# Interleaving the down products of two token tiles, and moving one subtraction from GpSimd to VectorE

## The chip, the core and the metric

The kernel runs on one core of a Trainium2 chip. A core has five engines with instruction queues of their own: TensorE (PE; its weight loads are listed apart as PEld), VectorE (DVE), ScalarE (ACT), GpSimd (POOL) and SyncE (SP), which here issues DMA transfers. Each engine takes its instructions in the order in which the program emits them and waits on semaphores for the others. The metric is the device time of one execution in microseconds (us), the median over the runs.

## What is computed

Four sequences of 512 tokens with 512 features; all in float32. For each sequence the features are normalised, and two branches read the result: attention with 16 heads of 32 (with RMS norm and rotation of queries and keys), and a gated feed-forward layer with 1408 hidden units. They are multiplied at the end:

```python
xn = _layernorm(x, axis=-1)
s = _L0_attn_ref(xn, L0_attn_w_qkv, L0_attn_w_out, L0_attn_q_gamma, L0_attn_k_gamma)
g = _silu(_L0_ffn_ref(xn, L0_ffn_wq_gate, L0_ffn_s_gate, L0_ffn_wq_up, L0_ffn_s_up, L0_ffn_wq_down, L0_ffn_s_down))
x = x + s * g
...
def _L0_ffn_ref(x, wq_gate, s_gate, wq_up, s_up, wq_down, s_down):
    gate = _qlinear(x, wq_gate, s_gate)
    gate = jax.nn.silu(gate)
    up = _qlinear(x, wq_up, s_up)
    return _qlinear(gate * up, wq_down, s_down)
```

The mask of the attention is causal. The feed-forward weights are integers, less a zero point and times a scale per row (`_qlinear`).

## The kernel before

The work is cut into 16 units (b, g): sequence b of 4 and head group g of 4 heads. The 11 hidden blocks of 128 are shared out over the four groups of a sequence: two to group 0, three to each of the others (`chunks`). A unit has two stages. The first, `hidden_window`, makes the unit's hidden blocks: for every block the gate product and the up product (`hidden`, L583, eight matmuls each), then `gate` and `gated`. Between them it does what is left of the last unit's attention, and in group 3 it turns the next sequence's normalised x. The second stage is the attention of the unit, and with it the down products of the blocks just made, one for each of the four token tiles of 128. The attention stage comes in three versions: `attention_window` for the first three units, `placed_window` for the next twelve, `last_window` for the last.

The order of the work is written out by hand: every engine's queue is the order of the calls, and nothing is moved afterwards. In the attention stage `s[t]` is the attention of token tile t. `scores` (L450) fills four PSUM banks; `probabilities` takes on VectorE the minimum of a row (L471) and on ScalarE the exponential (L481). `turn` transposes the probabilities on TensorE (L497) with a copy behind it (L125 on ScalarE, L127 on VectorE), `blocks` and `spread` do it with VectorE (L514) and DMA (L528). `values` (L537) multiplies by v. `fresh` is the projection of the next unit: `product` (L368), then `rotate`, which starts with two operations on ScalarE (L379, L380), goes on with four on VectorE (L400 to L407) and ends on GpSimd (L408, L314, L315, L410).

A float32 operand that is multiplied at the faster format is kept as two parts, a high half (rounded) and a low half (the rest). The hidden value has them in `h[:, i, 0]` and `h[:, i, 1]`. For one block, `gated` multiplies on VectorE (L600), makes the high half on ScalarE (L601) and the low half on GpSimd (L602). A down product of one token tile (`contract`, L612) is two matmuls per block, high then low, summed in one PSUM bank of 512 columns; `add` on VectorE (L623 for group 0, L625 for the others) adds the bank to `acc`. The first token tile uses the pool `ps_d`, of one bank, and so do the third and fourth; the second uses a bank of the pool of transposes (`bank_t`, two banks in turn). `contract` and the `add` that it returns are called separately, so that other work can stand between them.

The next sequence's x is cut in the same way into `xh` and `xl` by `Norm.cut`: ScalarE makes the high half (L350), another engine the low half (L351). It is called tile by tile through `halves`, in the attention stage of group 3 of sequences 0, 1 and 2. In `placed_window` GpSimd makes the low halves of tiles 0 and 1, VectorE those of 2 and 3.

Of the kernel before, what the change touches and what calls it, by code (L numbers as in the profile page):

```python
# [11 lines left out]
F32 = mybir.dt.float32  # L12
# [9 lines left out]
P = 128  # L22
B, N, D = 4, 512, 512
# [3 lines left out]
NC = D // P  # L27
# [24 lines left out]
def interleaved(  # L52
# [27 lines left out]
    nc = tc.nc  # L80
# [14 lines left out]
    ps_d = ctx.enter_context(tc.tile_pool(name="ps_d", bufs=1, space=PSUM))  # L95
# [8 lines left out]
    def bank_t(name):  # L104
        return ps_t.tile([P, 512], F32, tag="t", name=name)
# [33 lines left out]
    chunks = [list(range(first))] + [list(range(first + 3 * g, first + 3 * g + 3)) for g in range(NC - 1)]  # L139
# [42 lines left out]
    wdT = const.tile([P, NF, D], F32R, name="wdT")  # L182
# [50 lines left out]
    loaded, turning, finished = [], [], set()  # L233
# [74 lines left out]
    h = seq.tile([P, FC, 2, N], F32R, name="h")  # L308
# [288 lines left out]
    def gated(sil, f, bank, to):  # L597
# [3 lines left out]
        nc.scalar.copy(to[:, 0, :], sil)  # L601
        nc.gpsimd.tensor_tensor(to[:, 1, :], sil, to[:, 0, :].bitcast(F32), ALU.subtract)  # L602

    def contract(b, g, t, other=False):

        name = f"dn_{b}_{g}_{t}"
        bank = bank_t(name) if other else ps_d.tile([P, D], F32, tag="dn", name=name)
        fs = chunks[g]
        assert all(f"d_{m}_{f - f % 4}" in finished for m in range(NC) for f in fs)
        for i, f in enumerate(fs):  # L610
            for a in range(2):
                nc.tensor.matmul(  # L612
                    bank,
                    lhsT=h[:, i, a, ts(t, P)],
                    rhs=wdT[:, f, :],
                    start=(i == 0 and a == 0),
                    stop=(f == fs[-1] and a == 1),
                )

        def add():  # L620
            at = acc[:, t, :]
            if g == 0:
                nc.vector.tensor_copy(at, bank)  # L623
            else:
                nc.vector.tensor_tensor(at, bank, at, ALU.add)  # L625
            if (b, g) == units[-1]:
                nc.gpsimd.tensor_tensor(at, at, sdown, ALU.mult)

        return add
# [104 lines left out]
    def attention_window(b, g, last, s, fresh, norm):  # L734
# [19 lines left out]
        s[1].scores(s[0].whole, s[0].keys)  # L754
        s[0].probabilities(0, 1, 2, 3)
        add = contract(b, g, 0)
        s[1].probabilities(0)
        add()
        s[1].probabilities(1, 2, 3)
        if last is not None:  # L760
            last.divide()
        add = contract(b, g, 1, other=True)
        halves(0, 1)
        s[0].turn(0, scalar=False)
        project(0)
        add()
        rotate(0)
        beside(0)
        add = contract(b, g, 2)
        s[0].values()  # L770
        s[2].scores()
# [27 lines left out]
    def placed_window(b, g, last, s, fresh, norm, result):  # L799

        def halves(engine, *tiles):
            if norm is not None:
                for t in tiles:
                    norm.cut(t, engine)

        def beside(t):
            if result is not None:
                result.project(t)  # L810
                result.finish(t)

        def load(*tiles):
            if result is not None:
                for t in tiles:
                    result.load(t)

        load(0)
        s[0].scores()
        s[1].scores(s[0].whole, s[0].keys)  # L820
        s[0].probabilities(0, 1, 2, 3)
        if g == 0:
            fresh.product(0, other=True)
            fresh.square(0)
        add = contract(b, g, 0)
        s[1].probabilities(0, 1, 2, 3)
        add()
        if g == 0:
            fresh.rotate(0, squared=True)
        add = contract(b, g, 1, other=True)  # L830
        if last.placed:
            last.values()
        s[2].scores()
        add()
        s[2].probabilities(0, 1)
        add = contract(b, g, 2)
        s[0].turn(0, scalar=True)
        s[2].probabilities(2)
        s[1].turn(0, scalar=True)
        s[2].probabilities(3)  # L840
        s[1].turn(1, scalar=True)
        if g == 0:
            last.divide()
        s[2].blocks(0, 1, 2, 3)
        s[2].spread()
        load(1, 2)
        add()
        if g:
            last.divide()
        halves(nc.gpsimd, 0, 1)  # L850
        for t in range(NT):
            if t or g:
                fresh.product(t, other=t == NT - 1)
                fresh.rotate(t)
            if t == 1:
                halves(nc.vector, 2, 3)
            beside(t)
            if t == 1:
                load(3)
        for t in range(3):  # L860
            s[t].values()
        s[3].scores()
        s[3].probabilities(0, 1, 2, 3)
        contract(b, g, 3)()

    def last_window(b, g, last, s, result):


        turns.update(pr=0, pT=0)
        s[0].scores()  # L870
        s[1].scores(s[0].whole, s[0].keys)
        s[0].probabilities(0, 1, 2, 3)
        add = contract(b, g, 0)
        s[1].probabilities(0, 1, 2, 3)
        add()
        add = contract(b, g, 1, other=True)
        last.values()
        s[2].scores()
        add()
        s[2].probabilities(0, 1)  # L880
        add = contract(b, g, 2)
        last.divide()
        s[0].turn(0, scalar=True)
        s[2].probabilities(2)
        s[1].turn(0, scalar=True)
        s[2].probabilities(3)
        s[1].turn(1, scalar=False)
        add()
        s[0].values()
        s[1].values()  # L890
        s[3].scores()
        s[3].probabilities(0, 1)
        add = contract(b, g, 3)
        s[2].turn(0, scalar=False)
        s[3].probabilities(2)
        s[2].turn(1, scalar=False)
        s[3].probabilities(3)
        add()
        first, fourth = range(NT - 1), range(NT - 1, NT)
        s[3].spread_sums(first)  # L900
        s[3].spread_sums(fourth)
        for t in range(NT):
            result.gate(t)
        result.project(0, range(NC - 1))
        s[2].turn(2, scalar=False)
        s[2].turn(3, scalar=False)
        result.project(1, range(NC - 1))
        s[3].turn_sums(first)
        s[2].values()
        s[3].turn(0, scalar=False)  # L910
        s[3].divide(first)
        result.project(2, range(NC - 1))
        s[3].turn(1, scalar=False)
        result.project(0, range(NC - 1, NC))
        s[3].turn(2, scalar=True)
        result.finish(0)
        result.store(0)
        result.project(1, range(NC - 1, NC))
        s[3].turn_sums(fourth)
        s[3].turn(3, scalar=False)  # L920
        result.finish(1)
        result.store(1)
        result.project(2, range(NC - 1, NC))
        result.finish(2)
        result.store(2)
        s[3].values()
        s[3].divide(fourth)
        result.project(3, range(NC - 1))
        result.project(3, range(NC - 1, NC))
        result.finish(3, cut=True)  # L930
        result.store(3, cut=True)
# [37 lines left out]
    for u, (b, g) in enumerate(units):  # L969
# [26 lines left out]
        if swapped(b, g):  # L996
            placed_window(b, g, last, s, fresh, due, result)
        else:
            attention_window(b, g, last, s, fresh, due)
        last = s[3]  # L1000
    result = Result(B - 1)
    for t in range(NT):
        result.load(t)
    last_window(b, g, last, s, result)


# [425 lines left out]
def attn_times_ffn(tc: tile.TileContext, *args: bass.AP):  # L1432

    nc = tc.nc
    with tc.tile_pool(name="flag", bufs=1) as flag:
        wide = flag.tile([1, 1], I32, name="wide")
        interleaved(tc, *args, wide=wide)
        over = nc.values_load(wide, min_val=0, max_val=1)
        with tc.If(over != 0):
            in_float32(tc, *args)  # L1440
# [36 lines left out]
```

## Time and profile before

| | |
|---|---|
| time, median of 3 runs | 678.67 us (678.5 to 678.67) |
| the profiled execution | 679.54 us, span 677.7 us |
| instructions | 11804 |
| down products (L612) | 352 matmuls, 396 ns median of one |
| low halves of h (L602, GpSimd) | 44, 1287 ns median |
| low halves of x (L351) | 10 on GpSimd, 1278 ns median; 6 on VectorE, 682 ns median |
| adds of a down product to acc (L625, VectorE) | 48, 685 ns median |

The profile is of one execution. A line of the page's first part gives an engine's busy time, its share of the span and its instructions. The row PEclk gives in 40 slices of the span the clock that TensorE was granted, in tenths. Matmuls run into each other, so one lasts longer than the distance to the next. In the list of waits a line says which engine waited at which line of the kernel, for which engine and line, how long in all, how many times, and the longest. The chain of waits goes back from the last instruction, at each step to what released it. A line of the timeline has start, length, engine, line, operation, tiles and count; in brackets stands the idle time of the engine before it and what ended it ("issue" where the profile shows no wait).

### The profile page before, as it was taken

The numbers are of one execution on the slowest core, as the hardware profiler recorded it, in microseconds if no ns is written. First come the engines' busy times: TensorE is split into PE (matmuls) and PEld (weight loads), VectorE is DVE, ScalarE is ACT, GpSimd is POOL, SyncE is SP. The second block draws the span as 40 slices with busy tenths as digits, with TensorE's granted clock in tenths as the row PEclk, the third lists the DMA queues.
The fourth block names the chain that finished last, engine by engine and source line by source line (L and its number), as shares of the span: only waits on it lengthen the run. The fifth ranks groups of instructions, "written<-read, shape, count | busy, mean of one in ns | idle before, by whom it ended". The sixth has DMA issues, their size and how long they took to land.

```text
span 677.7 us, 11804 instructions
## 1 busy us (share of the span) xinstructions
PE 640.3 (94%) x4050; PEld 430.7 (64%) x4050; DVE 443.5 (65%) x1208; ACT 364.6 (54%) x931; POOL 319.9 (47%) x369
## 2 busy tenths in 40 slices
PE   4969999999999999999999999999999999999995
PEld 2645766668665576767665576766766466676752
DVE  3547677764886366777688357777588565757663
ACT  3456576554765064565757046464757246464660
POOL 4913536254472723537283641727284442726522
PEclk9969999999999999999999999999999999999998
DMA  7583644200222144322013323312223304222401
GB/s 250 149 209 94 180 97 107 94 1 1 48 55 68 50 124 100 74 47 46 22 43 79 94 44 106 102 46 48 64 47 78 94 1 125 47 63 48 125 1 68
DMA packets 48560, 53.19 MB, mean 78 GB/s; under 512 B 21334, under 2 KB 31852, under 8 KB 48492
## 3 DMA queue, kind: packets, MB, share of 16 engines
q1 hardware_dynamic: 47532, 51.93, 30.3%
q8 instruction: 34, 0.56, 0.3%
q10 hardware_dynamic: 960, 0.43, 0.2%
q14 instruction: 34, 0.28, 0.1%
HBM read 21.80 MB, written 4.19 MB: 38 GB/s over the span
## 4 chain that ended last, share of the span: by engine, by line
PE 84%; ACT 4%; DVE 4%; DMA 2%; POOL 2%; issue 2%; SPq 1%; DVEq 0%; ACTq 0%
PE qkv L368 25%; PE h L583 23%; PE dn L612 11%; PE so L655 8%; PE pv L537 6%; PE sc L450 5%; PE pt L497 4%; PE qkt L420 2%; POOL h L602 1%; DMA oT<-in_L_ffn_wq_up 1%; ACT arena L125 1%; DVE sil L600 1%; ACT arena L481 1%; PE xnt L344 1%; DMA x<-in_L_attn_x 1%
## 5 line engine op out<-in xcount | busy, mean ns | idle before, releaser
L481 ACT ACTIVATE arena<-arena,least 128x128 f32<-128x128 f32 (+3 forms) x256 | 141.2, 553 | 66.4 <-DVE least L471 66.3
L368 PE MATMUL qkv<-wqkv,xnT 128*128 128x384 f32 x512 | 173.6, 492 | 2.3 <-DVE least L471 2.3
L368 PEld LDWEIGHTS qkv<-wqkv,xnT 128*128 128x128 f32 x512 | 96.6, 193 | 68.6 <-issue 5.8
L471 DVE CUSTOM_DVE_ANT_0 arena<-sc,mask 128x128 f32<-128x128 f32 (+3 forms) x256 | 109.5, 486 | 31.0 <-PE sc L450 30.8
L408 POOL TENSOR_TENSOR qk<-qk,qs 128x256 f32<-128x256 f32 x64 | 46.7, 730 | 149.3 <-DVE qs L403 149.3
L602 POOL TENSOR_TENSOR h<-sil,h 128x512 fp32r<-128x512 f32 x44 | 57.8, 1314 | 116.2 <-ACT h L601 114.8
L315 POOL TENSOR_TENSOR ss<-ss,minus_half 128x8 f32<-128x8 f32 x64 | 106.7, 1668 | 5.3
L612 PE MATMUL dn<-wdT,h 128*128 128x512 f32 x352 | 100.0, 422 | 1.8 <-POOL h L602 1.8
L514 DVE STREAM_TRANSPOSE arena<-arena 128x384 f32<-128x384 f32 (+1 forms) x96 | 88.6, 977 | 12.3 <-PE pt L497 7.5
L612 PEld LDWEIGHTS dn<-wdT,h 128*128 128x128 f32 x352 | 63.5, 191 | 40.2 <-issue 20.4
L379 ACT ACTIVATE squares<-qkv 128x256 f32<-128x256 f32 x64 | 24.5, 382 | 119.7 <-PE qkv L368 99.0
L400 DVE TENSOR_TENSOR qk<-qkv,tab 128x256 f32<-128x256 f32 x64 | 27.0, 423 | 74.8 <-ACT v L380 74.4
L600 DVE SCALAR_TENSOR_TENSOR sil<-h,scales,sil 128x512 f32<-128x512 f32 x44 | 32.6, 740 | 56.8 <-PE h L583 45.0
L601 ACT CAST h<-sil 128x512 fp32r<-128x512 f32 x44 | 27.3, 620 | 69.8 <-DVE sil L600 69.8
L655 PE MATMUL so<-wout,oT 128*128 128x512 f32 x128 | 58.2, 593 | 0.0
L450 PE MATMUL sc<-kT,qT 32*128 32x512 f32 (+3 forms) x512 | 49.8, 474 | 5.8 <-ACT qT L125 5.8
L583 PE MATMUL h<-xh,wuT 128*128 128x512 f32 x176 | 50.1, 406 | 1.5 <-ACT qT L125 1.5
L497 PE MATMUL pt<-ident,arena 128*128 128x128 f32 x304 | 43.6, 279 | 7.2 <-ACT arena L125 7.1
L583 PE MATMUL h<-xh,wgT 128*128 128x512 f32 x176 | 49.1, 401 | 0.0
L497 PEld LDWEIGHTS pt<-ident,arena 128*128 128x128 f32 x304 | 35.0, 142 | 21.2 <-ACT arena L125 10.5
L583 PE MATMUL h<-xl,wuT 128*128 128x512 f32 x176 | 48.1, 395 | 0.0
L583 PE MATMUL h<-xl,wgT 128*128 128x512 f32 x176 | 48.1, 395 | 0.0
(90 smaller groups left out, 907.2 us busy)
## 6 DMA issues: line engine op xcount, KB each, us to landing
arena<-arena SPq DMA_DIRECT2D x48, 256.0 KB, 4.7
arena<-arena SPq DMA_DIRECT2D x48, 192.0 KB, 3.6
x<-in_L_attn_x SPq DMA_DIRECT2D x16, 256.0 KB, 4.7
out<-o SPq DMA_DIRECT2D x15, 256.0 KB, 4.5
xr<-in_L_attn_x SPq DMA_DIRECT2D x12, 256.0 KB, 4.1
wqkv<-in_L_attn_w_qkv SPq DMA_DIRECT2D x4, 576.0 KB, 4.8
wout<-in_L_ffn_wq_up SPq DMA_DIRECT2D x6, 256.0 KB, 3.1
wout<-in_L_ffn_wq_down SPq DMA_DIRECT2D x5, 256.0 KB, 3.9
```

Source lines behind the costliest of these rows:

```text
L315: nc.gpsimd.tensor_tensor(dst, dst, minus_half[:, : dst.shape[-1]], ALU.pow)
L368: nc.tensor.matmul(bank.rearrange("p (i d) -> p i d", i=3), lhsT=xnT[:, c, ts(t, P)], rhs=wqkv[:, c, :, self.g, :], start=(c == 0), stop=( ...
L408: nc.gpsimd.tensor_tensor(qk, qk, qs, ALU.add)
L450: nc.tensor.matmul(bank, lhsT=qT[rows, ts(self.t, P)], rhs=kT[rows, : self.keys], start=True, stop=True,)
L471: nc.vector.tensor_tensor_reduce(out=pr, in0=self.banks[j], in1=mask[:, N - self.keys :], scale=float(HD), scalar=3.0e38, op0=ALU.add, op1 ...
L481: nc.scalar.activation(pr, pr, AF.Exp, bias=least, scale=-1.0, accum_out=self.sums[:, self.t, j : j + 1],)
L497: nc.tensor.transpose(tp[:, ts(i * (self.t + 1) + k, P)], self.probs[n * self.per + i][:, ts(k, P)], ident,)
L514: nc.vector.transpose(piece(self.way, self.t + 1)[:, : HPG * self.keys].rearrange("p (c m k) -> p c m k", c=4, k=32)[:, :, j * n : (j + 1) * n
L583: nc.tensor.matmul(bank, lhsT=w[:, c, ts(f, P)], rhs=a[:, c, :], start=(c == 0 and a is xh), stop=(c == NC - 1 and a is xl),)
L602: nc.gpsimd.tensor_tensor(to[:, 1, :], sil, to[:, 0, :].bitcast(F32), ALU.subtract)
L612: nc.tensor.matmul(bank, lhsT=h[:, i, a, ts(t, P)], rhs=wdT[:, f, :], start=(i == 0 and a == 0), stop=(f == fs[-1] and a == 1),)
L655: nc.tensor.matmul(self.banks[t], lhsT=oT[:, g, ts(t, P)], rhs=wout[:, g, :], start=(g == 0), stop=(g == NC - 1),)
```

## The change

A new function `contract_two` does the down products of token tiles 0 and 1 together, in two banks: first all blocks but the last for tile 0, then for tile 1, then the last block for tile 0, then for tile 1. It takes the place of the first two calls of `contract` in `placed_window` and in `last_window`; `attention_window` keeps `contract`. Both banks are now taken, and all matmuls of both tiles issued, ahead of the call of `s[1].probabilities` and of the first add. The adds stay where they were in the order of calls; the closure that adds became the function `adding`. The second part is in `placed_window`: the low half of tile 1 of the next x is made by VectorE instead of GpSimd.

```diff
+    def contract_two(b, g):
+
+        banks = [ps_d.tile([P, D], F32, tag="dn", name=f"dn_{b}_{g}_0"), bank_t(f"dn_{b}_{g}_1")]
+        fs = chunks[g]
+        assert all(f"d_{m}_{f - f % 4}" in finished for m in range(NC) for f in fs)
+        for part in (fs[:-1], fs[-1:]):
+            for t, bank in enumerate(banks):
+                for f in part:
+                    for a in range(2):
+                        nc.tensor.matmul(
+                            bank,
+                            lhsT=h[:, f - fs[0], a, ts(t, P)],
+                            rhs=wdT[:, f, :],
+                            start=(f == fs[0] and a == 0),
+                            stop=(f == fs[-1] and a == 1),
+                        )
+        return [adding(b, g, t, bank) for t, bank in enumerate(banks)]
...
 # placed_window
-        add = contract(b, g, 0)
+        adds = contract_two(b, g)
         s[1].probabilities(0, 1, 2, 3)
-        add()
+        adds[0]()
         if g == 0:
             fresh.rotate(0, squared=True)
-        add = contract(b, g, 1, other=True)
         if last.placed:
             last.values()
         s[2].scores()
-        add()
+        adds[1]()
         s[2].probabilities(0, 1)
...
-        halves(nc.gpsimd, 0, 1)
+        halves(nc.gpsimd, 0)
+        halves(nc.vector, 1)
...
 # last_window
-        add = contract(b, g, 0)
+        adds = contract_two(b, g)
         s[1].probabilities(0, 1, 2, 3)
-        add()
-        add = contract(b, g, 1, other=True)
+        adds[0]()
         last.values()
         s[2].scores()
-        add()
+        adds[1]()
```

More of the change, by code (lines that the diff above doesn't have):

```diff
@@ L618, in contract, with adding @@
                 )
+        return adding(b, g, t, bank)
+    def adding(b, g, t, bank):
         def add():
```

## The prediction

> **What bounds the kernel now.** I read the page first, then the list of waits, then the chain of waits and the timeline around single pairs of down products. Below, a window is named by its sequence (0 to 3) and head group (0 to 3); a block is one of the two or three hidden blocks of 128 that a window contracts.
>
> ```profile
> PE 640.3 (94%) x4050; PEld 430.7 (64%) x4050; DVE 443.5 (65%) x1208; ACT 364.6 (54%) x931; POOL 319.9 (47%) x369
> PEclk9969999999999999999999999999999999999998
> PE 84%; ACT 4%; DVE 4%; DMA 2%; POOL 2%; issue 2%; SPq 1%; DVEq 0%; ACTq 0%
> ```
>
> TensorE is busy 94% of the span at full granted clock and has 84% of the chain. So time is won only where TensorE stands still, or lost where it is made to. From the list of waits (who waited for whom: us in all, times, longest), those of the weight loads (PEld) and of VectorE's adds:
>
> ```profile
> PEld dn L612 <- POOL h L602: 5.2, 9, 0.7
> DVE acc L625 <- PE dn L612: 4.2, 9, 0.6
> DVE acc L623 <- PE dn L612: 3.5, 4, 1.0
> ```
>
> Down products wait nine times for POOL's low half of h. VectorE's own waits for down products, 7.7 us in 13, are small. The chain of waits in the window of sequence 1, group 1 (start, us, what):
>
> ```profile
> 249.36 0.76 DVE sil L600
> 250.14 0.63 ACT h L601
> 250.84 1.30 POOL h L602
> 252.18 1.90 PE dn L612 x7
> ```
>
> The last hidden block goes DVE, ACT, POOL before TensorE may go on. The timeline's weight loads of that pair, and of one where POOL is not late (sequence 1, group 3); in brackets the idle before and its releaser:
>
> ```profile
> 250.48 1.00 PEld L612 LDWEIGHTS dn<-wdT,h 128*128 128x128 f32 x5 [0.33 <-issue]
> 252.17 1.47 PEld L612 LDWEIGHTS dn<-wdT,h 128*128 128x128 f32 x7 [0.69 <-POOL h L602]
> 254.01 0.81 PEld L537 LDWEIGHTS pv<-arena,v 128*32 128x32 f32 x32 [0.37 <-issue]
> ...
> 325.59 1.00 PEld L612 LDWEIGHTS dn<-wdT,h 128*128 128x128 f32 x5 [0.33 <-issue]
> 326.77 1.46 PEld L612 LDWEIGHTS dn<-wdT,h 128*128 128x128 f32 x7 [0.17 <-POOL h L602]
> 328.59 0.48 PEld L537 LDWEIGHTS pv<-arena,v 128*32 128x32 f32 x20 [0.36 <-issue]
> ```
>
> Five loads pass (four of the first two blocks, and the high half of the third), the sixth stops. Twelve loads take 254.01 - 250.48 = 3.53 us with the stop and 328.59 - 325.59 = 3.00 us without; the idle before the sixth is 0.69 against 0.17. Both say 0.52 to 0.53 us lost. Nine waits of 5.2 us in all are seven of 0.69 to 0.70 and two of 0.17, and these two cost nothing. The timeline shows the seven: groups 1 and 2 of sequences 1, 2 and 3 (loads stopped until 252.17, 288.76, 409.60, 446.16, 567.01 and 603.59 us), and the last window (640.14).
>
> **The change part by part.** *The weave.* The number of matmuls and weight loads stays; only their order changes. In a window of three blocks it becomes: first tile blocks 1 and 2 (four matmuls), second tile the same (four), first tile block 3 (two), second tile block 3 (two). The first one that needs POOL's last low half is now the tenth instead of the sixth. At a pitch of 0.233 us (24 hidden matmuls in 5.60 us) the sixth load, unhindered, falls at 252.17 - 0.52 = 251.65 and the tenth at 251.65 + 4 x 0.233 = 252.58. POOL ends at 250.84 + 1.30 = 252.14: covered by 0.44 us. The ninth needs ScalarE's high half, over at 250.77. The cover is the second tile's four matmuls, 0.93 us; if they were not ready, the 0.52 us would be back. They need the bank that the last up product left, read by VectorE until 250.12, well ahead of the fifth load. In windows of group 0 that bank is left by ScalarE's copy of the reciprocals, over at 203.19, and the second tile's first load, here the third, comes at about 204.06; in windows of group 3 by ScalarE's copy of xnT, over at 325.83, needed at 326.5. No new wait there. Saving: 7 x 0.53 = 3.7 us. The other six pairs (three of group 0, three of group 3) lose nothing now and win nothing.
>
> *What is late next.* VectorE's first add waits for the tenth matmul instead of the sixth; in its queue stand the second add and the third tile's minima. Ends at 254.08 - 0.53 = 253.55 for the pair put the tenth's end at about 253.09. The add ran at 252.80 straight behind the minima, now at 253.13: +0.33. The second add ran at 254.12 and now at 253.73 (a pitch of 0.60 behind the first), ending at 254.42. The first score of the third tile comes at 255.97 - 0.53 = 255.44, so VectorE still waits there, by 1.0 us. In group 0 the first add goes from position 4 to 6, +0.47 (205.11 to 205.58), in front of a wait of 1.52 us for ScalarE before the next operation; its third product needs the bank only at 207.72. In group 3 it is +0.3 to +0.4, and ends in sequence 0 at the latest at 173.11 where the minima begin at 173.13: nothing, but without room.
>
> ScalarE decides whether the 0.53 us comes through: a few lines below, TensorE waits for its copy at the transposes of the probabilities.
>
> ```profile
> 256.57 0.62 ACT L481 ACTIVATE arena<-arena,least 128x384 f32<-128x384 f32 x1 [0.39 <-DVE least L471]
> 258.03 0.58 ACT L125 COPY arena<-pt 128x512 f32<-128x512 f32 x1 [0.15 <-PE pt L497]
> 258.67 0.66 PE L497 MATMUL pt<-ident,arena 128*128 128x128 f32 x4 [0.24 <-ACT arena L125]
> ```
>
> ScalarE is solid from 250.66 to 256.18 and has 0.39 + 0.15 = 0.54 us of slack ahead of that copy, just the size of the saving. So the copy comes 0.53 us earlier, and the projections (10.3 us of TensorE without a gap) with it. Value taken 0.53; the lower end is 0.39 if the second slack is no slack, the upper 0.69 if the whole idle goes.
>
> *Low halves of one tile.* Three windows (group 3 of sequences 0 to 2). POOL loses one operation of 1.26 us, VectorE gets one at 0.64 us in a row (pairs take 1.28), so 1.9 us of VectorE in all. It stands ahead of the first rotation. ScalarE's high half is over at 178.96 while VectorE arrives at 180.65: no wait. The first two rotations come 0.64 us later; ScalarE's squares of tile 2 waited 0.81 us for TensorE and still do by 0.1 to 0.2; the rotation of tile 3 waits 1.43 us for ScalarE, so VectorE is back in step there. The projections' banks are read by 186.34 and wanted at 188.25. POOL doesn't gain: it waited 0.52 us for VectorE after its two operations, and now starts its row of rotations 0.64 us later, ending at 195.98 instead of 195.34; TensorE loads the first of these tiles at 196.12 and the fourth, which is the late one, at about 196.5. Cost 0, with 0.5 us of cover. No step is moved on SP's queue; no DMA is issued earlier or later but with its producers.
>
> [...] The row first: POOL's multiplication L410 takes 0.99 us where VectorE does low halves beside it, 0.62 elsewhere. [...] the new operation may cost POOL 0.37 us a window, 1.1 us in all; by the trace POOL is idle then (its one operation ends near 179.8), and the 0.99 moves along unchanged. I take 0; even with it, 196.35 is before 196.5. The second: 24 hidden matmuls in three banks run in 5.60 us, 0.233 each, with no gap at the bank's change, and the clock in every such stretch is 1.00. [...] I take the row: the banks already change here without loss.
>
> **Sum.** The profiled execution took 679.54 us, 1.84 beyond its span, and 0.87 above the median of 678.67. 679.54 - 3.7 = 675.8 for it; on the median 678.67 - 3.7 = 675.0.
>
> **The rivals.**
>
> *ScalarE takes over part of the wait.* Its row of exponentials is solid before the copy; if only 0.39 us comes through, 7 x 0.39 = 2.7: 676.0. For it: the slack is as large as the saving to 0.01 us. Against: the 0.15 us is a wait for TensorE itself.
>
> *The wait only moves.* TensorE stands at the transposes for as long as it stood at the down products: 678.7. For it: the wait for ScalarE's copy is in every window (10.5 us of weight loads in all). Against: the copy's own last wait is for TensorE.
>
> *VectorE's queue becomes the bound.* The first adds come later by 7 x 0.33 + 3 x 0.37 + 3 x 0.47 = 4.8 us, the new operations add 1.9; if none of it were hidden, 6.7 - 3.7 = +3.0: 681.7. It decides once the second add ends behind the third tile's first score (1.0 us away in the seven windows, near 0 in group 3 of sequence 0), or POOL's last rotation behind 196.5. Against it are the measured waits that VectorE still has behind each of these places.
>
> That the change does nothing of what it says can be left aside: it is plain in the order of matmuls.
>
> **How the numbers follow.** The weave works as worked out, 0.70: 675.0, own range 674.2 to 675.9. ScalarE keeps part, 0.10: 676.0, down to 677. The wait only moves, 0.08: 678.7. VectorE's queue, 0.12: 681.7. About 0.2%, 1.4 us, is what a measurement tells from no change. Faster is the first two, 0.80; same 0.08; slower 0.12. The lower end takes most of the 0.69 us bound (7 x 0.69 = 4.8 would be 673.9); the upper takes in the partial gain. Range 674.0 to 677.0.
>
> **What would show it.** Right: the wait of dn for POOL h gone or at 0.17 each; twelve loads of a pair in about 3.0 us in groups 1 and 2; the wait of DVE acc for dn larger (by some 0.3 us a window); the wait at pt for ScalarE's copy unchanged; L351 seven on POOL, nine on VectorE, and no new wait at qkt. Wrong: pt's wait up by 0.5 us in seven windows, a wait of the third tile's minima for acc, a qkt wait for POOL after group 3, or a granted clock below 1.00 in the pairs.

## The result, and the profile after

The changed kernel takes 674.8 us (median of 7 runs, 674.39 to 677.45) against 678.67 us before (7 runs, 677.74 to 678.96). The ratio over all the runs is 0.9951, with a 95% interval of 0.9937 to 0.9965: faster by 0.35 to 0.63%. The profiled execution took 675.08 us with a span of 673.3 us. That is 4.46 us below the one before: 3.7 us come in the seven windows of the prediction, 0.3 us lie ahead of all of them (the wait of the first transposes for x is 9.1 us instead of 9.4), and 0.4 us behind the start of the last stores. The last two belong to single executions; the medians differ by 3.9 us.

From the page (engines, granted clock, chain by engine):

```profile
PE 638.2 (95%) x4050; PEld 431.2 (64%) x4050; DVE 445.2 (66%) x1211; ACT 363.9 (54%) x931; POOL 316.3 (47%) x366
PEclk9979999999999999999999999999999999999998
PE 87%; ACT 4%; DVE 3%; DMA 2%; issue 1%; SPq 1%; POOL 0%; DVEq 0%; ACTq 0%
```

The counts of matmuls and loads are the same. POOL's share of the chain, 2% before, is 0%; TensorE's busy time fell by 2 us although it does the same work: of the seven waits of before, the profile listed 1.8 us as idle time of PE and counted the rest as busy. From the list of waits (us in all, times, longest), what is left of the woven down products (L613; the others are L630 now) and of the adds behind them (L644, L646):

```profile
PEld dn L613 <- issue: 3.3, 10, 0.3
DVE acc L644 <- PE dn L613: 3.9, 3, 1.3
DVE acc L646 <- PE dn L613: 2.1, 8, 0.3
```

The row of 5.2 us for POOL h is gone. Next, the chain of waits in sequence 1, group 1, and then the timeline's weight loads there and in group 3 of the same sequence:

```profile
249.37 0.87 PE sc L450 x16
250.24 3.00 PE dn L613 x12
253.23 1.01 PE pv L537 x32
```

```profile
250.16 2.63 PEld L613 LDWEIGHTS dn<-wdT,h 128*128 128x128 f32 x12 [0.33 <-issue]
253.16 0.81 PEld L537 LDWEIGHTS pv<-arena,v 128*32 128x32 f32 x32 [0.37 <-issue]
...
324.22 2.63 PEld L613 LDWEIGHTS dn<-wdT,h 128*128 128x128 f32 x12 [0.33 <-issue]
327.21 0.81 PEld L537 LDWEIGHTS pv<-arena,v 128*32 128x32 f32 x32 [0.37 <-issue]
```

DVE, ACT and POOL have left the chain ahead of the down products. The twelve loads take 3.00 us in both windows (3.53 and 3.00 before). The starts of the pairs show the sum growing. Start before less start after is 0.32 us at the first pairs (169.18 and 250.48 against 168.86 and 250.16). At the eight later pairs of groups 1 to 3 it is 0.86, 1.37, 1.35, 1.88, 2.40, 2.40, 2.95 and 3.47. So there are steps of 0.51 to 0.55 behind groups 1 and 2, and none behind group 3 or group 0. The last window adds 0.53: the last store starts at 668.61 instead of 672.63.

### The profile page after: what moved, and what is told of

Read it like the earlier page. It is cut to its first block, busy times and chain, and to the rows that moved or that the text cites. A ratio compares the mean times of both kernels' runs of the same rounds, so it can differ in the third digit from the quotient of the medians.

```text
span 673.3 us, 11804 instructions
## 1 busy us (share of the span) xinstructions
PE 638.2 (95%) x4050; PEld 431.2 (64%) x4050; DVE 445.2 (66%) x1211; ACT 363.9 (54%) x931; POOL 316.3 (47%) x366
## 4 chain that ended last, share of the span: by engine, by line
PE 87%; ACT 4%; DVE 3%; DMA 2%; issue 1%; SPq 1%; POOL 0%; DVEq 0%; ACTq 0%
PE qkv L368 25%; PE h L583 23%; PE so L676 8%; PE dn L630 7%; PE sc L450 6%; PE pv L537 6%; PE dn L613 5%; PE pt L497 4%; PE qkt L420 2%; DMA oT<-in_L_ffn_wq_up 1%; ACT arena L125 1%; ACT arena L481 1%; PE xnt L344 1%; PE rt L561 1%; DMA x<-in_L_attn_x 1%
## 5 line engine op out<-in xcount | busy, mean ns | idle before, releaser
L630 PE MATMUL dn<-wdT,h 128*128 128x512 f32 x208 | 60.5, 427 | 0.0
L630 PEld LDWEIGHTS dn<-wdT,h 128*128 128x128 f32 x208 | 37.9, 193 | 26.4 <-issue 16.0
L497 PEld LDWEIGHTS pt<-ident,arena 128*128 128x128 f32 x304 | 35.0, 142 | 21.2 <-ACT arena L125 10.5
```

Source lines behind the costliest of these rows:

```text
L497: nc.tensor.transpose(tp[:, ts(i * (self.t + 1) + k, P)], self.probs[n * self.per + i][:, ts(k, P)], ident,)
L630: nc.tensor.matmul(bank, lhsT=h[:, i, a, ts(t, P)], rhs=wdT[:, f, :], start=(i == 0 and a == 0), stop=(f == fs[-1] and a == 1),)
```

## The experiments

The theory was the prediction's: TensorE's wait for GpSimd's last low half in seven windows is all of it, 7 x 0.53 us; the moved subtraction is worth nothing. The rivals: the moved subtraction gives part of it, the order gives something in all 13 windows for another reason, VectorE's or ScalarE's queue takes part back. All times are medians; a ratio is over all the runs, to the kernel before on the same chip. That kernel took 678.49 us beside the first four experiments, 678.47 beside the doublings, the single VectorE operation and the earlier copies, and 677.8 beside the other three.

**One part alone.** First the new order with the old placing of the low halves:

```diff
-        halves(nc.gpsimd, 0)
-        halves(nc.vector, 1)
+        halves(nc.gpsimd, 0, 1)
```

> The new order of the down products, with the low halves of tiles 0 and 1 of the next x both on GpSimd as before. Theory (TensorE's wait for GpSimd's last low half in seven pairs is the whole of it, 7 x 0.53 us): 3.7 us below the kernel before, 675.0, the same as the full change within 0.5 us. Rival (the move of the subtraction gives part of it, by relieving GpSimd in three windows): about 676 to 677.

Measured: 674.78 us, ratio 0.9942 (0.9928 to 0.9956). Then the kernel before with the other part only (the same two lines, the other way):

> The old order of the down products, with the low half of tile 1 moved to VectorE. Theory: no effect, 678.7 within 0.5 us; GpSimd's row of rotations starts 0.6 us later in three windows and the transposes of q and k still don't wait. Rival (VectorE's queue is the bound): 3 x 0.64 = 1.9 us slower, 680.6. Rival (GpSimd is relieved): up to 1 us faster.

Measured: 678.25 us, ratio 0.9996 (0.9989 to 1.0002). The whole gain is in the order. What the moved subtraction does is seen in POOL's timeline of this second run (sequence 1, group 3) beside the weight loads behind it:

```profile
334.52 1.29 POOL L351 TENSOR_TENSOR xl<-xnT,xh 128x512 fp32r<-128x512 f32 x1 [9.23 <-ACT xh L350]
338.21 0.73 POOL L408 TENSOR_TENSOR qk<-qk,qs 128x256 f32<-128x256 f32 x1 [2.40 <-DVE qs L403]
```

```profile
352.12 1.03 PEld L420 LDWEIGHTS qkt<-ident,qk 128*128 128x128 f32 x8
353.86 0.76 PEld L583 LDWEIGHTS h<-xh,wuT 128*128 128x128 f32 x4 [0.71 <-ACT qT L125]
```

POOL has one operation less and waits 2.40 us for VectorE instead of 0.52: it was not short of time, it was waiting for the engine that now has more to do. The transposes of q and k, which need POOL's last rotation, load without a wait, and the wait behind them is the 0.7 us of before.

**The windows without a wait.** The new order only in the six windows where GpSimd is not late (the last window has the old order too, and the low halves of x are made as before):

```diff
+        woven = g in (0, 3)
+        adds = contract_two(b, g) if woven else [contract(b, g, 0)]
...
+        if not woven:
+            adds.append(contract(b, g, 1, other=True))
```

> The new order only in the six windows of groups 0 and 3 in which GpSimd is not late; groups 1 and 2 and the last window keep the old order; low halves as before. Theory: nothing to win there, 678.7 within 0.5 us. Rival (the new order is worth something in each of the 13 windows, for another reason than the wait): 6/13 of the gain, 1.8 us faster, 676.9. Rival (the first add, later by 0.3 to 0.5 us, pushes VectorE's queue): up to 2.5 us slower, 681.2.

Measured: 678.23 us, ratio 0.9996 (0.999 to 1.0002). In these windows the order by itself is worth nothing, and the later first add costs nothing.

**The wait taken away without the order.** The old order, but the first two token tiles read the first block's low half in place of the late one (the result is then another, the number of matmuls is not):

```diff
-                    lhsT=h[:, i, a, ts(t, P)],
+                    lhsT=h[:, 0 if a and t < 2 and (b, g) >= units[NC - 1] else i, a, ts(t, P)],
```

> The old order, but the down products of tiles 0 and 1 in the 13 windows read the first block's low half in place of every other block's, so that part of the computation is changed: TensorE needs nothing of GpSimd's last low half there, which is still made. Theory: the seven waits go, 3.7 us faster, 675.0, and this is all that the new order can win. Rival (the order matters beyond that wait): less than half of it, 677 or above.

Measured: 675.02 us, ratio 0.9944 (0.9929 to 0.996). Its twelve loads at the pair of sequence 1, group 1:

```profile
250.49 2.63 PEld L612 LDWEIGHTS dn<-wdT,h 128*128 128x128 f32 x12 [0.33 <-issue]
```

The same 2.63 us busy in one piece as with the new order. The same replacement in the changed kernel:

> The changed kernel in which the woven down products read the first block's low half in place of every other block's, so that part of the computation is changed and no matmul there needs GpSimd's last low half. Theory: the new order covers all of that wait already: 674.8 within 0.7 us. Rival (some of the wait is left at the tenth matmul): faster by up to 1 us or more, 673.8.

Measured: 674.74 us, ratio 0.9957 (0.9941 to 0.9974). Two ways to be rid of the wait give the same time, and both together give no more. So the wait is the whole of what was won.

**How large the cover is.** The late operation doubled, in the old order and in the new:

```diff
+        if twice:
+            nc.gpsimd.tensor_tensor(to[:, 1, :], sil, to[:, 0, :].bitcast(F32), ALU.subtract)
...
-            gated(sil, f, bank, h[:, i])
+            gated(sil, f, bank, h[:, i], f == chunks[g][-1] and (b, g) >= units[NC - 1])
```

> The kernel before, with the last block's low half made twice on GpSimd (same values) in the 13 windows, 1.27 us more of it each time. Theory: with the old order there is no cover left, so the seven pairs lose 1.27 us each (8.9), two of group 3 1.24 (2.5), the third 0.3 and group 0 at most 0.3 each: 11.7 to 12.6 us slower, about 690.5. Rival (only part of such a wait reaches the end, since ScalarE takes it over): 6 us or less, 684 or below.

> The changed kernel, with the same doubling. Theory: the tenth load stands 0.44 us behind GpSimd's end, so 0.83 us of the 1.27 comes through in seven pairs (5.8), 0.3 in two of group 3 (0.6), nothing in the others: 6.4 us slower than the changed kernel, 681.2; against the doubling in the old order 9.5 us less. Rival (the new order's cover is all of the second tile's work, or POOL is not what the loads wait for): no more than 2 us slower, 676.8.

Measured: 691.19 us in the old order, ratio 1.0196 (1.0179 to 1.0212), 12.7 us above the kernel before: without cover nearly all of it comes through. (The loads' waits grew from 5.2 to 18.8 us, and the medians by 12.7.) In the new order 682.96 us, ratio 1.0061 (1.0049 to 1.0073). From the timeline of the second, again sequence 1, group 1 (L604 is the repeated operation):

```profile
250.45 1.93 PEld L615 LDWEIGHTS dn<-wdT,h 128*128 128x128 f32 x9 [0.33 <-issue]
253.51 0.54 PEld L615 LDWEIGHTS dn<-wdT,h 128*128 128x128 f32 x3 [1.13 <-POOL h L604]
```

```profile
250.81 1.30 POOL L602 TENSOR_TENSOR h<-sil,h 128x512 fp32r<-128x512 f32 x1 [2.45 <-ACT h L601]
252.18 1.28 POOL L604 TENSOR_TENSOR h<-sil,h 128x512 fp32r<-128x512 f32 x1
```

The wait is now at the tenth load; nine pass. Of its 1.13 us, 0.17 are the idle time that stands there anyway, so 0.96 us are lost, and unhindered the tenth would come at 252.55. GpSimd's first operation ends at 252.11: cover 0.44 us, as worked out. The run was expected 6.4 us above the changed kernel and came 682.96 - 674.8 = 8.2 above it. The traces show 7 x 0.96 us, and 0.62 - 0.17 = 0.45 in group 3 of sequences 1 and 2, so 7.6 in all. That much of the miss, 1.2 us, is the operation's distance: the second one ends at 253.46, 1.35 us behind the first and not 1.27, and the load follows by 0.05. The other 0.6 us is in no wait at the down products.

**VectorE's room.** One and three operations behind the second add:

```diff
         adds[1]()
+        for _ in range(1):   # 3 in the second run
+            nc.vector.tensor_tensor(acc[:, 1, :], acc[:, 1, :], acc[:, 1, :], ALU.max)
         s[2].probabilities(0, 1)
```

> The changed kernel with one more VectorE operation of 0.6 us (a maximum of acc with itself, no effect on values) behind the second add in the 12 middle windows. Theory: VectorE has 1.03 us of room behind it in the six windows of groups 1 and 2 and in two of group 3: nothing. In group 0 of three sequences, where ScalarE waits for VectorE there, 0.6 each, and in the first of group 3 about 0.5: 2.3 us slower than the changed kernel, 677.1. Rival (no room anywhere): 12 x 0.6 = 7.2 slower, 682. Rival (room everywhere): 674.8.

> The changed kernel with three more VectorE operations of 0.6 us behind the second add in the 12 middle windows. Theory: 1.8 us pass the room of 1.03 us in the six windows of groups 1 and 2 and two of group 3 by 0.7 each (5.6), all of it comes through in three of group 0 (5.4) and 1.7 in the first of group 3: 12.7 us slower than the changed kernel, 687.5. Rival (room is larger than the idle time shows, since TensorE is the bound): 680 or below.

Measured: 677.47 us with one, ratio 0.9989 (0.9979 to 1.0), so 2.7 us above the changed kernel where 2.3 was expected; 695.78 us with three, ratio 1.0272 (1.0251 to 1.0293), 21 us above it where 12.7 was expected. VectorE with one more in sequence 1, group 1:

```profile
254.10 1.29 DVE L646 TENSOR_TENSOR acc<-dn,acc 128x512 f32<-128x512 f32 x2 [0.24 <-PE dn L613]
255.43 0.69 DVE L856 TENSOR_TENSOR acc<-acc 128x512 f32<-128x512 f32 x1
256.42 0.56 DVE L471 CUSTOM_DVE_ANT_0 arena<-sc,mask 128x384 f32<-128x384 f32 x1 [0.30 <-PE sc L450]
```

Of 1.03 us of room 0.30 are left, and TensorE's wait for ScalarE's copy stays at 0.47 us in this window. In group 0 of sequence 1 it grew from 1.80 to 2.53 us: there VectorE has no room. With three operations the waits at that copy grow from 10.5 to 26.6 us of weight loads in all, 16.1 more, where 12.7 were expected. Two things make up these 3.4 us. Three operations in a row, each on the result of the last, take 2.15 us and not 1.8. And the room is not 1.03 us everywhere. In group 2 of sequences 1 and 2 VectorE also works on the next sequence's x (L328, L329), comes late to the adds, and has 0.32 us left in the changed kernel (sequence 1):

```profile
289.54 1.28 DVE L646 TENSOR_TENSOR acc<-dn,acc 128x512 f32<-128x512 f32 x2
291.15 0.56 DVE L471 CUSTOM_DVE_ANT_0 arena<-sc,mask 128x384 f32<-128x384 f32 x1 [0.32 <-PE sc L450]
```

In these two windows the wait for the copy grew by 1.50 us under the three operations, and by 0.80 in the six that had 1.03 us of room. The rest of the miss comes from TensorE's clock and is told in the last section.

**The next wait.** What TensorE meets below the woven products is the copy of the transposed probabilities. ScalarE's copies one exponential earlier:

```diff
-        s[2].probabilities(0, 1)
+        s[2].probabilities(0)
         add = contract(b, g, 2)
         s[0].turn(0, scalar=True)
-        s[2].probabilities(2)
+        s[2].probabilities(1)
         s[1].turn(0, scalar=True)
-        s[2].probabilities(3)
+        s[2].probabilities(2)
         s[1].turn(1, scalar=True)
+        s[2].probabilities(3)
```

> The changed kernel with ScalarE's three copies of transposed probabilities each put one exponential earlier in the 12 middle windows (the transposes stay where they are among TensorE's matmuls). The next wait of TensorE is the one for the first of these copies: 0.48 us of weight loads in 9 windows, 1.8 us in the 3 of group 0. Theory: 0.25 to 0.4 us a window in 9, 0.6 in 3: 4 to 5 us faster than the changed kernel, 670.3. Rival (the third tile's exponentials, now later, hold up VectorE's transposes or the rotations and give it back): 674.8 or above.

Measured: 673.27 us, ratio 0.9919 (0.9906 to 0.9932): 1.5 us below the changed kernel, where 4 to 5 were expected. Sequence 1, group 1:

```profile
255.80 0.59 ACT L125 COPY arena<-pt 128x512 f32<-128x512 f32 x1 [0.70 <-PE pt L497]
256.43 0.42 PEld L497 LDWEIGHTS pt<-ident,arena 128*128 128x128 f32 x4 [0.47 <-ACT arena L125]
```

In group 0 the wait fell from 1.80 to 1.20 us, 3 x 0.6 = 1.8 us. In the other nine windows ScalarE now stands 0.66 to 0.74 us for the transposes, and TensorE waits 0.47 as before. So ScalarE's row doesn't set the wait there. The explanation put to the test next: two transposed groups fill both banks, and the third needs the first one's copied out. The first transposes were put ahead of the third tile's down product, whose six matmuls run while the bank is copied:

```diff
+        if g:
+            s[0].turn(0, scalar=True)
         s[2].probabilities(0)
         add = contract(b, g, 2)
-        s[0].turn(0, scalar=True)
+        if g == 0:
+            s[0].turn(0, scalar=True)
         s[2].probabilities(1)
```

> The changed kernel, with the copies one exponential earlier as in the run before, and in the nine windows outside group 0 the first transposes of probabilities (four matmuls) ahead of the third tile's down product instead of behind it. Theory: TensorE's wait of 0.48 us at the third group of transposes is the time in which a bank is copied (two banks in turn), and six down matmuls cover it: 9 x 0.3 to 0.4 us less[...]: 1.5 to 3.5 us below 673.3, about 671. Rival (ScalarE's row is what sets it, so the same wait is met later): 673.3.

Measured: 668.2 us, ratio 0.986 (0.9843 to 0.9876), 1.4% below the kernel before and the fastest here. Weight loads of sequence 1, group 1:

```profile
253.33 0.42 PEld L497 LDWEIGHTS pt<-ident,arena 128*128 128x128 f32 x4 [0.55 <-ACT arena L481]
253.72 1.23 PEld L630 LDWEIGHTS dn<-wdT,h 128*128 128x128 f32 x6
255.00 1.03 PEld L497 LDWEIGHTS pt<-ident,arena 128*128 128x128 f32 x8
```

The 0.47 is gone, and no new idle came with the move: the 0.55 us that stood ahead of the down product now stand ahead of the transposes, and the next two changes, to the down product and back, show none. With the 0.67 us between the two medians of the kernel before taken off, this version is 673.27 - 668.2 - 0.67 = 4.4 us below the last one, 0.49 a window: the whole wait, more than the 1.5 to 3.5 us expected.

## Why the prediction was right

- **Which wait, and what it is worth**: 0.53 us in seven windows, 3.7 us. The traces show steps of 0.51 to 0.55. Taking away only the wait gave 3.5 us, only the order 3.7.
- **The order costs nothing in itself**: the third experiment shows it, 678.23 us against 678.49. In the profile of the changed kernel the granted clock is 1.00 in the stretch of each of the 13 woven pairs, and twelve matmuls, with three changes of bank instead of one, still take 3.00 us (sequence 1, groups 1 and 3).
- **Cover 0.44 us at the tenth load**: measured by the doubling.
- **ScalarE lets it through**: the copy started 257.17 - 250.16 = 7.01 us behind the first load, and 258.03 - 250.48 = 7.55 before. All 0.54 us came through, and the rival with 0.39 was left with nothing. The 0.15 us in front of the copy had been a wait for TensorE's transposes, and these came earlier too. That the saving just fitted is in part luck: only 0.10 us of ScalarE's idle time is left ahead of the copy (257.07 to 257.17), so a much larger saving would not have come through whole.
- **The moved subtraction costs nothing**: right in time. POOL's multiplication of 0.99 us still takes 0.99; the new operation ran while POOL stood (in sequence 1 at 336.72 for 0.66 us, POOL idle from 335.84 to 338.19). Two details were off by little. ScalarE's squares of tile 2 wait 0.26 us for VectorE's sums, where 0.1 to 0.2 us of waiting for TensorE was to be left. The rotation of tile 3 waits 0.97 us where 1.43 stood before, so the later start has been made up there as the text said.
- **VectorE's adds**: in sequence 1, group 1, the first waits 0.24 us (0.33 worked out as its delay). That the list of waits would show more was wrong in the sum: 7.7 us before and after, since the second add's wait of 0.63 us went as the first one's came.

One reading did not hold, and it cost nothing here. The rival with VectorE's queue as the bound put the distance of the second add from the third tile's first score at 1.0 us in the seven windows. It is 1.03 us in five of them and 0.32 in the other two, group 2 of sequences 1 and 2. The prediction read it off sequence 1, group 1, where VectorE has no statistics of the next x to make. In the other two the room was 0.85 us before, and the saving itself took 0.53 of it. For group 0 the prediction said that a wait of 1.52 us hides the later add. It does: that wait was 1.06 us after. But behind it, at the second add, VectorE has no room at all, which the run with one more operation shows.

## What to carry to other kernels

When the last of several producers is late, and two consumers each need it at the end of their sums, open both sums at once and let each one's early terms stand ahead of the late one; here it cost a bank and no time (678.23 us against 678.49 where there was no wait to win). Find the late one by the idle ahead of a weight load, less the idle that the same load has where nothing is late (0.69 against 0.17 us here), and check what the first consumer's later end holds up. Before relieving an engine, look at what it waits for: here it waited for the engine that was to take its work, and nothing came of it. Read the slack of an engine in every window that is to use it; windows of the same shape differed by 0.7 us.

## What was not expected of the hardware

In the run with three more VectorE operations TensorE lost more than its waits. The timeline around the stall of group 0 in sequence 1:

```profile
213.56 1.12 PE L497 MATMUL pt<-ident,arena 128*128 128x128 f32 x4 [3.74 <-ACT arena L125]
214.47 6.10 PE L676 MATMUL so<-wout,oT 128*128 128x512 f32 x8
```

The table by stretches at the same place (us; busy time and count of PE, PEld, DVE, ACT and POOL; PEclk; DMA share; GB/s):

```profile
212.00:212.50 0.50, 0.00 (x0) 0.00 (x0) 0.50 (x3) 0.50 (x3) 0.00 (x0) 1.00 0.00 0
212.50:213.00 0.50, 0.00 (x0) 0.00 (x0) 0.50 (x3) 0.50 (x3) 0.00 (x0) 0.67 0.00 0
214.00:216.00 2.00, 2.00 (x6) 1.15 (x5) 1.64 (x3) 1.66 (x6) 0.00 (x0) 0.50 0.00 0
```

TensorE stood from 213.56 - 3.74 = 209.82. The granted clock went to half while it stood, at 212.67 (0.67 is the mean of its stretch), and came back at 219.49. Eight output products took 6.10 us; at full clock, after the same stall of 3.74 us in sequence 3, they took 3.60 (0.43 us apart; the hidden matmuls, of 512 columns too and in the faster format, come 0.233 us apart in this run):

```profile
542.35 0.66 PE L497 MATMUL pt<-ident,arena 128*128 128x128 f32 x4 [3.74 <-ACT arena L125]
542.84 3.60 PE L676 MATMUL so<-wout,oT 128*128 128x512 f32 x8
```

So the same stall cost the clock in sequences 1 and 2 (half from 376.5 to 383.3, worked out from the means of the stretches; eight products in 5.75 us) and not in sequence 3, where every stretch from 526 to 552 us has 1.00. Both stretches at half clock last 6.8 us. When the clock fell, TensorE had stood for 2.85 us in sequence 1 and for 376.5 - 374.37 = 2.1 us in sequence 2; in sequence 3 it stood for 3.74 us and kept the clock. So the length of the stall alone did not settle it, and what did is not shown.

A stall of 2.29 us at this place, in the run with one operation, left the clock at 1.00 in the execution that was profiled (209 to 220 us). But three of that run's 22 executions took 680.9 to 681.4 us with a mean clock of 0.985 to 0.987, where the others have 0.989 to 0.994. One stretch of 6.8 us at half clock would lower the mean by 0.005 (an estimate), so a stall of 2.29 us may sometimes have cost the clock too. No trace of these three is kept: that is not shown.

The two drops cost 2.5 + 2.15 us at the output products and 0.9 at the transposes ahead of them, 5.6 us. With the 16.1 us of waits, and less the 1.5 us that this execution had gained before its first woven pair, that makes 20.2 us; its span grew by 20.4. The wait grew dearer by a step: in the changed kernel TensorE stands 1.56 us at this place, and the 2.2 us more of this run cost 2.2 us in sequence 3 and some 5 us in the other two.
